# Linear attention and a sparse feed-forward layer: the gate products of token blocks two to four by two levels of seven products

## The chip, the cores and the metric

One core of one Trainium2 chip runs the kernel. The metric is the device time of one execution in microseconds (us); the kernel is run three times and the median is given. The engines are TensorE (PE in the profile; PEld are its weight loads), VectorE (DVE), ScalarE (ACT), GpSimd (POOL) and SyncE (SP), whose queue issues nearly all transfers. Each engine works through its instructions in the order in which they were written.

## The reference

Two stages with a residual each, on 2 x 1024 tokens of width 512, all in float32. The change is in the second.

```python
x = L0_attn_x                                     # (2, 1024, 512)
x = x + _layernorm(_L0_attn_ref(_layernorm(x), Wq, Wk, Wv, Wo))
x = x + _layernorm(_L0_ffn_ref(_layernorm(x), w_gate, w_up, w_down))

def _L0_ffn_ref(x, w_gate, w_up, w_down):         # (512, 2048), (512, 2048), (2048, 512)
    h = silu(einsum('bsh,hi->bsi', x, w_gate)) * einsum('bsh,hi->bsi', x, w_up)
    h_sparse = _sparsify_2to4(h)                  # of each 4 neighbours keep the 2 of largest |h|
    return einsum('bsi,ih->bsh', h_sparse, w_down)
```

`_L0_attn_ref` is a causal linear attention with 16 heads of 128 channels.

## The kernel before

The first 650 us are the attention, chunk by chunk of 128 tokens; the change leaves its code as it is. Then comes the feed-forward stage in four blocks of 512 tokens (`m` = 0 to 3; the text counts them from one). A block's hidden layer of 2048 is computed in four sets of 512 columns (`jb` = 0 to 3). For each set there is a `gate` and an `up`, both 512 x 512 x 512; after the four sets there is one `down`, 512 x 2048 x 512.

**Seven products.** Each of these matrix products is made by seven products of half the size in each direction in place of eight (a scheme of Strassen's kind). `FACTORS` says which of the seven combined weights meets which of the seven combined inputs. Three of the weight factors are quarters of the weight itself; the other four were summed ahead, by POOL in the attention stage, and lie in DRAM (`gu_dram`, `d_dram`). The inputs are combined by DVE and POOL (`ffn_input`, lines 1998 to 2005, tile `fxt`; `sparsify`, lines 1785 to 1794, tile `ht`).

`chain` (line 630) makes the seven products in the order 1, 2, 6, 5, 7, 4, 3. Products 1, 6, 7 and 4 add up in one PSUM bank (kind `b`); in between ACT copies the bank to SBUF (`snapshot`, line 659). Product 2 has a bank of kind `a`; 5 and 3 share one of kind `e`. DVE adds `a` or `e` to a snapshot to finish a quarter of the result (`added`, line 672). The fourth quarter is read from bank `b` itself. There are two banks of kind `a` and three each of `b` and `e`. For a gate or an up, one of the seven products is four matmuls with 128x128 weights and 256 moving columns (`project_ffn`, line 364); for a down it is sixteen (line 1811).

**After the products.** ACT applies Silu to the gate's quarters (`gate`, lines 1668 to 1678). `sparsify` multiplies gate and up on DVE, takes absolute values on ACT (line 1743), compares and counts on DVE (lines 1749 to 1775) and keeps two of four (line 1779), some 13 us of DVE for a set. The three differences of tile `ht` and one POOL sum (line 1794) make the factors for down.

**Order.** `Plan` orders the instructions. TensorE's are written out by hand in `ffn_order`; everything else is a process that names its engine and a length in us (`yield "dve", 0.7`), and the plan simulates them and writes each engine's instructions in the order it found. Lengths are constants: that one engine slows another is not in them. `weave` alternates between a gate and an up of the same or the next set. In down, products 1, 2 and 5 are split: part one uses sets 0 to 2, part two set 3, which is selected last.

**Between blocks.** Before, all seven products of the second block's first gate are run within or right after the first block's last gate and up products, or between the parts of down. At the change from the second block to the third no gate product stands between them, and at the next change two do. The input of block `m` is normalized one block ahead (`ffn_normalized`), transposed by DVE and through DRAM (`ffn_input`, `fb_dram`), and held in two tiles that alternate (`xs`, `xo`), so that it is loaded a block ahead.

**Buffers.** `ring` holds 12 gate or up factors of 256 KB each; `wd` holds 4 down factors of 1024 KB; `fx` holds the blocks' residual inputs until the output is written (`write_output`).

Of the kernel before, what the change touches and what calls it, by code (L numbers as in the profile page):

```python
# [17 lines left out]
P = 128  # L18
# [201 lines left out]
def layer(  # L220
# [47 lines left out]
    gu_dram = [[dram.tile([P, 4, 512], F32, name=f"{of}s{jb}") for of in "gu"] for jb in range(NJB)]  # L268
    d_dram = dram.tile([P, NJB, 4, 512], F32, name="d_dram")
# [53 lines left out]

    def load_x2(m):
# [18 lines left out]
    def load_gu(jb, which, i):  # L343

        t = pool["ring"].tile([P, 2, 2, P], F32, tag="gu", name="wgu")
        f = FACTORS[i][0]
        h, m = QUARTERS[f]
        if f < 3:
            of = columns((w_gate, w_up)[which], jb)
            v = of.rearrange("p (h k) (j m c) -> p h k j m c", h=2, j=2, m=2)  # L350
        else:
            of = gu_dram[jb][which]
            v = of.rearrange("p (h k) (j m c) -> p h k j m c", h=2, j=2, m=2)
        for k in range(2) if f < 3 else [slice(0, 2)]:
            nc.sync.dma_start(out=t[:, k], in_=v[:, h, k, :, m, :])
        return t
# [21 lines left out]
    def down_factor(i):  # L378
        wi = FACTORS[i][0]
        w = pool["wd"].tile([P, NJB, 2, 256], F32, tag="wd", name="wd")  # L380
        h, m = QUARTERS[wi]
        if wi < 3:
            of = w_down.rearrange("(b p h k) (m c) -> p b h k m c", b=NJB, h=2, k=2, m=2)
        else:
            of = d_dram.rearrange("p b (h k) (m c) -> p b h k m c", h=2, m=2)
        for k in range(2):
            nc.sync.dma_start(out=w[:, :, k], in_=of[:, :, h, k, m, :])
        return w
# [241 lines left out]
    def chain(name, shape, length, product, names, keeps, c11, c12, c22, c21, last=None):  # L630
# [113 lines left out]
        plan.signal((*name, 3))  # L744
        yield
# [708 lines left out]

    def begin_ffn():

        for name, bufs in (("ring", 12), ("fx", 4), ("ln", 4), ("xs", 1), ("keeps", 4), ("s", 2)):
# [7 lines left out]
        first_ups = [(0, i) for i in ORDER] + [(1, i) for i in ORDER[:5]]  # L1465

        def first_gates():
# [3 lines left out]
            for jb, i in first_ups:  # L1471
                wgu_loaded.add((0, jb, 1, i))
                yield from load_factor(0, jb, 1, i)

        def normalized():
            yield 6.0
            scales = yield from layernorm_pair(ffn["x"], 4, "f4", None)
            for tt in range(4):
                yield "dve", 0.56
                xn = pool["ln"].tile([P, NIC, P], F32, tag="ln", name="fxn")  # L1480
                normalize(xn.rearrange("p c d -> p (c d)"), ffn["x"][tt], *scales[tt])
                ffn["xn"][tt] = xn
# [5 lines left out]
    def ffn_transposed(tt, kind):  # L1488
# [4 lines left out]
        pt, name = transposed(ffn["xn"][tt], kind, ("fxn", tt))  # L1493
# [34 lines left out]
    def load_factor(m, jb, which, i):  # L1528
        before, name = ring("gu", 12)
        yield from before  # L1530
        if FACTORS[i][0] > 2:
            yield "unit", 5 + 2 * jb + which
        yield "sp", 0.88 if FACTORS[i][0] < 3 else 0.44, 2
# [770 lines left out]
```

## Time and profile before

| | |
|---|---|
| median of three runs | 1267.67 us (1266.99 to 1269.98) |
| the profiled execution's time | 1267.78 us |
| its span, first to last instruction | 1266.1 us |
| granted TensorE clock | 0.998 |
| first gate product, last matmul group begins | 664.95 us, 1252.68 us |
| transfers | 252.60 MB, mean 200 GB/s |

The groups of lines that the change is near, from the list of the costliest groups (columns: line, engine, operation, tile written <- tiles read, shape, count | busy us, mean ns of one | idle before, and what ended it):

```profile
L364 PE MATMUL cb<-fxt,wgu 128*128 128x256 f32 x512 | 116.7, 380 | 1.0 <-ACT u L659 0.6
L659 ACT COPY u<-cb 128x512 f32<-128x512 f32 (+1 forms) x252 | 126.5, 502 | 432.9 <-PE cb L364 157.6
L1794 POOL TENSOR_TENSOR h<-h 128x512 f32<-128x512 f32 x16 | 26.1, 1636 | 303.2 <-DVE ht L1791 123.6
wgu<-gs SPq DMA_DIRECT2D x64, 256.0 KB, 3.6
wgu<-us SPq DMA_DIRECT2D x64, 256.0 KB, 3.1
wd<-d_dram SPq DMA_DIRECT2D x32, 512.0 KB, 5.0
```

A float32 matmul leaves two records, so 512 records of line 364 are 256 matmuls. Records overlap: the mean of one (380 ns) is from its start to its last result, and the next has begun before. What one costs is read from start to start.

### The profile page before, as it was taken

The numbers are of one execution on the slowest core, as the hardware profiler recorded it, in microseconds if no ns is written. First come the engines' busy times: TensorE is split into PE (matmuls) and PEld (weight loads), VectorE is DVE, ScalarE is ACT, GpSimd is POOL, SyncE is SP. The second block draws the span as 40 slices with busy tenths as digits, with TensorE's granted clock in tenths as the row PEclk, the third lists the DMA queues.
The fourth block names the chain that finished last, engine by engine and source line by source line (L and its number), as shares of the span: only waits on it lengthen the run. The fifth ranks groups of instructions, "written<-read, shape, count | busy, mean of one in ns | idle before, by whom it ended". The sixth has DMA issues, their size and how long they took to land. (4 is left out here: it accounts for less than half of the span.)

```text
span 1266.1 us, 17832 instructions
## 1 busy us (share of the span) xinstructions
PE 1247.5 (99%) x6092; PEld 990.1 (78%) x6092; DVE 850.9 (67%) x1577; ACT 464.5 (37%) x911; POOL 336.5 (27%) x263
## 2 busy tenths in 40 slices
PE   7999999999999999999999999999999999999998
PEld 4666776777767776777688888888888888888886
DVE  6898877876666677777764499227872698237763
ACT  3664454443443444444543333013411333023211
POOL 4554443332422455455421110010100101010010
PEclk9999999999999999999999999999999999999999
DMA  7377867769758776766575688376547775565312
GB/s 267 109 229 255 270 187 238 236 221 291 230 187 262 250 238 229 243 203 223 185 230 167 179 228 233 116 218 207 156 149 211 230 198 146 166 181 169 108 42 92
DMA packets 280297, 252.60 MB, mean 200 GB/s; under 512 B 19216, under 2 KB 239376, under 8 KB 277520
## 3 DMA queue, kind: packets, MB, share of 16 engines
q1 hardware_dynamic: 278832, 249.51, 63.6%
q10 hardware_dynamic: 1376, 1.97, 0.4%
q8 instruction: 49, 0.80, 0.3%
q14 instruction: 40, 0.33, 0.1%
HBM read 179.83 MB, written 71.57 MB: 199 GB/s over the span
## 5 line engine op out<-in xcount | busy, mean ns | idle before, releaser
L659 ACT COPY u<-cb 128x512 f32<-128x512 f32 (+1 forms) x252 | 126.5, 502 | 432.9 <-PE cb L364 157.6
L1234 ACT ACTIVATE o<-nm,den 128x128 f32<-128x128 f32 x256 | 81.5, 367 | 120.4 <-DVE den L1228 81.1
L1331 PE MATMUL cb<-wo,of 128*128 128x256 f32 x512 | 123.5, 384 | 0.6 <-ACT u L659 0.6
L883 PE MATMUL cb<-wq,xf 128*128 128x512 f32 x256 | 121.9, 598 | 0.0
L928 POOL TENSOR_TENSOR qraw<-qraw,r 128x512 f32<-128x512 f32 x48 | 62.8, 1308 | 213.7 <-DVE qraw L919 163.6
L364 PE MATMUL cb<-fxt,wgu 128*128 128x256 f32 x512 | 116.7, 380 | 1.0 <-ACT u L659 0.6
L364 PE MATMUL cb<-fxnT,wgu 128*128 128x256 f32 x512 | 116.8, 379 | 0.0
L1331 PEld LDWEIGHTS cb<-wo,of 128*128 128x128 f32 x512 | 93.6, 190 | 21.1 <-issue 8.2
L364 PEld LDWEIGHTS cb<-fxt,wgu 128*128 128x128 f32 x512 | 97.0, 190 | 15.1 <-ACT u L659 1.3
L364 PEld LDWEIGHTS cb<-fxnT,wgu 128*128 128x128 f32 x512 | 97.2, 190 | 13.3
L1794 POOL TENSOR_TENSOR h<-h 128x512 f32<-128x512 f32 x16 | 26.1, 1636 | 303.2 <-DVE ht L1791 123.6
L565 POOL TENSOR_TENSOR wraw<-wraw 128x512 f32<-128x512 f32 x68 | 95.5, 1404 | 2.4
L672 DVE TENSOR_TENSOR y<-u,ce 128x256 f32<-128x256 f32 (+1 forms) x42 | 18.9, 451 | 97.8 <-ACT u L659 65.0
L883 PEld LDWEIGHTS cb<-wq,xf 128*128 128x128 f32 x256 | 47.2, 190 | 44.7 <-issue 42.8
L883 PEld LDWEIGHTS cb<-wkv,xf 128*128 128x128 f32 x256 | 48.0, 192 | 31.7 <-issue 25.3
L883 PE MATMUL cb<-wkv,xf 128*128 128x256 f32 x256 | 68.2, 389 | 0.0
L1331 PE MATMUL ce<-wo,of 128*128 128x256 f32 x256 | 60.5, 379 | 0.0
L883 PE MATMUL ce<-wq,xf 128*128 128x512 f32 x128 | 60.2, 592 | 0.0
L364 PE MATMUL ca<-fxnT,wgu 128*128 128x256 f32 x256 | 58.8, 379 | 0.0
L364 PE MATMUL ce<-fxt,wgu 128*128 128x256 f32 x256 | 58.7, 379 | 0.0
L364 PE MATMUL ce<-fxnT,wgu 128*128 128x256 f32 x256 | 58.7, 379 | 0.0
L1811 PE MATMUL cb<-wd,h 128*128 128x256 f32 x256 | 57.3, 379 | 0.0
(189 smaller groups left out, 2415.6 us busy)
## 6 DMA issues: line engine op xcount, KB each, us to landing
wgu<-gs SPq DMA_DIRECT2D x64, 256.0 KB, 3.6
wgu<-us SPq DMA_DIRECT2D x64, 256.0 KB, 3.1
wd<-d_dram SPq DMA_DIRECT2D x32, 512.0 KB, 5.0
qb<-blocks SPq DMA_DIRECT2D x59, 256.0 KB, 2.3
qT<-qb SPq DMA_DIRECT2D x236, 64.0 KB, 2.6
ob<-blocks SPq DMA_DIRECT2D x58, 256.0 KB, 3.2
of<-ob SPq DMA_DIRECT2D x232, 64.0 KB, 2.5
xf<-xf SPq DMA_DIRECT2D x16, 896.0 KB, 5.4
```

Source lines behind the costliest of these rows:

```text
L364: nc.tensor.matmul(bank[:, j, :].rearrange("p (w t) -> p w t", t=32), w[:, k, j, :], xf[xi][:, k], start=(start and j == 0 and k == 0), st ...
L565: nc.gpsimd.tensor_tensor(to, i0, i1, op)
L659: nc.scalar.copy(kept[i], b)
L672: nc.vector.tensor_tensor(dst[:, rows], kept[i][:, rows], b, ALU.add)
L883: nc.tensor.matmul(bank.rearrange("p h d -> p (h d)"), xf[n][:, xi, k, :], w[wi][:, k, :], start=(start and k == 0), stop=(k == 1), skip_g ...
L928: nc.gpsimd.tensor_tensor(u, u, r, ALU.add)
L1234: nc.scalar.activation(t[:, u, :], nmv[:, u // 2, u % 2, 0:HD], AF.Copy, scale=den[:, u // 2, u % 2 : u % 2 + 1],)
L1331: nc.tensor.matmul(bank.rearrange("p h d -> p (h d)"), of[n, xi][:, k, :], weights[gp][2][wi][:, k, :], start=(start and k == 0), stop=(k ...
L1794: nc.gpsimd.tensor_tensor(b12, b22, b12, ALU.subtract)
L1811: nc.tensor.matmul(b[:, j if row is None else 0, :], hts_or_h(m, jb, hi)[:, k, j * P : (j + 1) * P], w[:, jb, k, :], start=(start and part ...
```

## The change

For the gates of blocks two to four (12 of 16) each of the seven products is made by seven products again: `inner_gate` uses `chain_of_chains` in place of `chain`. A product that was four matmuls of 256 columns becomes seven matmuls of 128 columns, their results in two PSUM banks (four in the first, three in the second). Snapshots and sums of the outer level hold seven 128-column results in place of four (tile `u2`, three buffers). When an outer quarter is complete, POOL makes its four inner quarters from the seven results by five additions (`post`); Silu follows.

The inner combinations of the weights are made by POOL from the outer factors: in block one, as the third and fourth gate's factors are loaded there, and for the first and second set after them (`inner_weights`, `more_inner_weights`); they are stored to DRAM (`gi_dram`), and an inner gate loads three quarters of the outer factor and the four inner sums, 448 KB in place of 256. The inner combinations of the input are 12 more DVE instructions per block (`inner`).

For their room other buffers are cut: `ring` holds 7 up factors and 4 larger gate factors, `wd` holds 3, and the fifth down factor is loaded to the two `fx` tiles; these no longer keep the residual, which is loaded again just before it is added (`residual`). The transposed input has one buffer, so it is loaded after the last gate and up product of the block before. `ht` has two places: its third difference overwrites the second after down's product 6. In `sparsify` the sums of the comparisons are reordered and partly written over the comparisons. Between blocks, eight of down's steps now run first, then the next gate's products 1 and 2 with down's last two between, then the first of the next up.

```diff
+    gi_dram = [dram.tile([P, 7, 4, P], F32, name=f"gi{jb}") for jb in range(NJB)]
...
+        if some:
+            nc.sync.dma_start(out=to[:, 0, 0, :], in_=v[:, 0, 0, :])
+            nc.sync.dma_start(out=to[:, 1], in_=v[:, 1])
+            return
...
+        t = pool["ring"].tile([P, 8, P], F32, tag="gi", name="wgi", bufs=GI)
+        v = t[:, 0:4].rearrange("p (k j) c -> p k j c", k=2)
+        load_blocks(v, jb, which, i, inner)
+        if inner:
+            nc.sync.dma_start(out=t[:, 4:8], in_=gi_dram[jb][:, FACTORS[i][0]])
+            return t
+        return v if which else (t[:, 4:8], v)
...
+        if i == 5:
+            ts = []
+            for b in range(2):
+                t = pool["fx"].tile([P, B, DM], F32, tag="fx", name="fx")
+                t = t.rearrange("p b (k c) -> p b k c", k=2)
+                for k in range(2):
+                    nc.sync.dma_start(out=t[:, :, k], in_=of[:, 2 * b : 2 * b + 2, h, k, q, :])
+                ts += [t[:, 0], t[:, 1]]
+            return ts
...
+    SLOTS = (1, 2, 6, 5, 7, 4, 3)
+    PARTS = (slice(0, 4), slice(4, 7))
...
+        def multiply(bs, i, start, more=None):
+            for part, (b, _, before) in enumerate(bs):
+                plan.pe(
+                    (0.89, 0.67)[part],
+                    partial(product, b, i, part, start),
+                    *names(i),
+                    *(before if start else [(*name, *more, part)]),
+                )
+            plan.signal((*name, i))
...
+        def snapshot(bs, i, last=False):
+            yield from taken(i)
+            for part, of_ in enumerate(PARTS):
+                yield "act", (0.62, 0.5)[part], 0
+                src = bs[part][0] if part == 0 else bs[part][0][:, 0:3]
+                nc.scalar.copy(kept[i][:, of_], src)
+                plan.signal(bs[part][1] if last else (*name, "kept", i, part))
+            if last:
+                yield from post(i, quads[i])

+        def added(i, bs, last):
+            for part, of_ in enumerate(PARTS):
+                yield (*name, "kept", i, part)
+                yield "dve", (0.73, 0.6)[part], 0
+                t = kept[i][:, of_]
+                src = bs[part][0] if part == 0 else bs[part][0][:, 0:3]
+                nc.vector.tensor_tensor(t, t, src, ALU.add)
+                plan.signal(bs[part][1] if last else (*name, "e", part))
+            yield from post(i, quads[i])
+
+        def post(i, quad):
+            begin, d, then = quad
+            yield from begin
+            d = d()
+            if i == 1:
+                plan.signal((*name, "begun"))
+            t = kept[i]
+            for length, to, i0, i1 in (
+                (0.8, d[:, 0], t[:, 0:1].broadcast_to([P, 2, P]), t[:, 1:3]),
+                (0.5, d[:, 1, 1], d[:, 0, 1], t[:, 4]),
+                (0.5, d[:, 1, 0], d[:, 1, 1], t[:, 5]),
+                (0.8, d[:, :, 1], d[:, :, 1], t[:, 3:4].broadcast_to([P, 2, P])),
+                (0.5, d[:, 0, 1], d[:, 0, 1], t[:, 6]),
+            ):
+                yield "pool", length
+                nc.gpsimd.tensor_tensor(to, i0, i1, ALU.add)
+            plan.signal(free[i])
+            yield from then()
...
+        b = banks("b")
+        multiply(b, 1, True)
+        plan.spawn(snapshot(b, 1))
+        yield
+        a = banks("a")
+        multiply(a, 2, True)
+        plan.spawn(added(1, a, True))
+        yield
+        multiply(b, 6, False, ("kept", 1))
+        plan.spawn(snapshot(b, 6))
+        yield
+        e = banks("e")
+        multiply(e, 5, True)
+        yield
+        multiply(b, 7, False, ("kept", 6))
+        plan.spawn(snapshot(b, 7))
+        plan.spawn(added(7, e, False))
+        yield
+        multiply(b, 4, False, ("kept", 7))
+        plan.spawn(snapshot(b, 4, True))
+        yield
+        multiply(e, 3, False, ("e",))
+        plan.spawn(added(6, e, True))
...
+    def inner_weights(jb, i, v, done):
+
+        t, v = v
+        yield "gu", 0, jb, 0, i
+        (a11, a21), (a12, a22) = ([v[:, k, j, :] for j in range(2)] for k in range(2))
+        s4, s2, s3, s1 = (t[:, k] for k in range(4))
+        for to, i0, i1, op in (
+            (s1, a21, a22, ALU.add),
+            (s2, s1, a11, ALU.subtract),
+            (s3, a11, a21, ALU.subtract),
+            (s4, a12, s2, ALU.subtract),
+        ):
+            yield "pool", 0.5, 2
+            nc.gpsimd.tensor_tensor(to, i0, i1, op)
+        yield "sp", 0.44, 2
+        nc.sync.dma_start(out=gi_dram[jb][:, FACTORS[i][0]], in_=t)
+        yield plan.transfer(256)
+        done()
+        plan.signal(("gi", jb, i))
+
+    def more_inner_weights():
+        yield "g", 0, 3, 7
+        for jb in range(2):
+            for i in ORDER:
+                t, name = yield from take("keep2", 3, new_keep2)
+                if FACTORS[i][0] > 2:
+                    yield "unit", 5 + 2 * jb
+                yield "sp", 0.88 if FACTORS[i][0] < 3 else 0.44, 2
+                v = t[:, 0:4].rearrange("p (k j) c -> p k j c", k=2)
+                load_blocks(v, jb, 0, i)
+                plan.spawn(landed(plan.transfer(256), ("more", jb, i)))
+                plan.spawn(inner_weights(jb, i, (t[:, 3:7], v), partial(plan.signal, name)))
...
-            if m == 0:
-                run(g, 4)
-            else:
-                g = gate(m + 1, 0)
-            if m != 1:
-                for part in range(2):
-                    run(products, 1)
-                    run(g, 1)
-            run(products, 8 if m == 1 else 6)
-            u = up(m + 1, 0)
-            for part in range(2):
-                if m == 1:
-                    run(g, 1)
-                run(u, 1)
-                run(products, 1)
-            live += [u] if m == 0 else [g, u]
+            run(products, 8)
+            g, u = gate(m + 1, 0), up(m + 1, 0)
+            run(g, 1)
+            run(products, 1)
+            run(g, 1)
+            run(products, 1)
             begin(m + 1)
+            run(u, 1)
+            live += [g, u]
...
+    def load_fifth(m):
+        for tt in range(4):
+            yield "fxn", min(m + 1, NM - 1), tt
+        yield from load_down_factor(m, 5, ("wd more", m))
...
+        def product(bank_, i, part, start):
+            w, name = wgu[m, jb, 0, i]
+            xi = FACTORS[i][1]
+            x_ = xfs[m][xi]
+            o_ = (0, 1, 3, 4, 5, 2, 6)[xi]
+            places = SLOTS[PARTS[part]]
+            for n, j in enumerate(places):
+                wj, xj = FACTORS[j]
+                if xj < 3:
+                    k, t_ = ((0, 0), (1, 0), (1, 1))[xj]
+                    rhs = x_[:, k, 4 * t_ : 4 * t_ + 4]
+                else:
+                    rhs = xis[m][:, xj - 3, o_].rearrange("p (w t) -> p w t", t=32)
+                nc.tensor.matmul(
+                    bank_[:, n, :].rearrange("p (w t) -> p w t", t=32),
+                    w[:, (0, 2, 3, 5, 4, 6, 7)[wj], :],
+                    rhs,
+                    start=(start and n == 0),
+                    stop=(n + 1 == len(places)),
+                    skip_group_check=True,
+                )
+            if part:
+                del wgu[m, jb, 0, i]
+                plan.signal(name)
...
+                1: (before, quad(0, 0, new), first_rows),
+                6: (begun, quad(0, 1), rows),
+                7: (begun, quad(1, 1), c22),
+                4: (begun, quad(1, 0), c21),
...
-        n = pool["m"].tile([P, 4, 512], BF16, tag="n", name="n")
-        for k, first, second, op in (
-            (0, g0[:, 0, :], g0[:, 1, :], ALU.add),
-            (0, n[:, 0, :], g0[:, 2, :], ALU.add),
-            (1, g1[:, 0, :], g0[:, 0, :], ALU.subtract),
-            (1, n[:, 1, :], g1[:, 1, :], ALU.add),
-            (2, g2, g0[:, 1, :], ALU.subtract),
-            (2, n[:, 2, :], g1[:, 0, :], ALU.subtract),
-            (3, g2, g1[:, 1, :], ALU.add),
-            (3, n[:, 3, :], g0[:, 2, :], ALU.add),
+        n0 = pool["m"].tile([P, 512], BF16, tag="n", name="n")
+        n = [n0, g0[:, 0, :], g0[:, 1, :], g2]
+        for to, first, second, op in (
+            (n[0], g0[:, 0, :], g0[:, 1, :], ALU.add),
+            (n[0], n[0], g0[:, 2, :], ALU.add),
+            (n[1], g1[:, 0, :], g0[:, 0, :], ALU.subtract),
+            (n[2], g2, g0[:, 1, :], ALU.subtract),
+            (n[3], g2, g1[:, 1, :], ALU.add),
+            (n[1], n[1], g1[:, 1, :], ALU.add),
+            (n[2], n[2], g1[:, 0, :], ALU.subtract),
+            (n[3], n[3], g0[:, 2, :], ALU.add),
...
-        t = pool["h"].tile([P, 3, 2, 256], F32, tag="ht", name="ht")
-        hts[m, jb] = [b11, b21, b22, t[:, 0], t[:, 1], b12, t[:, 2]]
-        for k, i0, i1 in ((0, b12, b11), (1, b22, t[:, 0]), (2, b21, t[:, 1])):
+        t = pool["h"].tile([P, 2, 2, 256], F32, tag="ht", name="ht")
+        hts[m, jb] = [b11, b21, b22, t[:, 0], t[:, 1], b12, t[:, 1]]
+        for k, i0, i1 in ((0, b12, b11), (1, b22, t[:, 0])):
             yield "dve", 0.7
             nc.vector.tensor_tensor(t[:, k], i0, i1, ALU.subtract)
         plan.signal(("ht", m, jb))
+
+        def third():
+            yield "d", m, 6
+            yield "dve", 0.7
+            nc.vector.tensor_tensor(t[:, 1], b21, t[:, 1], ALU.subtract)
+            plan.signal(("ht4", m, jb))
+
+        plan.spawn(third())
...
-            if m > 1:
-                yield "gu done", m - 2
+            yield "gu done", m - 1
             for b in range(4):
                 yield "sp", 0.44
                 if not xnT:
-                    of_ = pool["xs" if m % 2 == 0 else "xo"]
-                    xnT.append(of_.tile([P, 16, NIC, 32], F32, tag="fxnT", name="fxnT"))
+                    xnT.append(pool["xs"].tile([P, 16, NIC, 32], F32, tag="fxnT", name="fxnT"))
...
+        def inner(o_, count, part):
+            to = [
+                xis[m][:, k, o_ : o_ + count].rearrange("p i (w t) -> p i w t", t=32)
+                for k in range(4)
+            ]
+            for k, i0, i1 in (
+                (0, part(0, 1), part(0, 0)),
+                (1, part(1, 1), to[0]),
+                (2, part(1, 1), part(0, 1)),
+                (3, part(1, 0), to[1]),
+            ):
+                yield "dve", 0.15 + count * 0.15, 0
+                nc.vector.tensor_tensor(to[k], i0, i1, ALU.subtract)
+            plan.signal(("fxi", m, o_ // 2))
...
-        fxs[0] = ffn["x"]
         actx.close()
-        for name, bufs in (("wd", 4), ("h", 4), ("m", 1), ("y", 1), ("blocks", 2), ("xo", 1)):
+        for name, bufs in (("wd", 3), ("h", 4), ("m", 1), ("y", 1), ("blocks", 2), ("xi", 1), ("keep2", 3)):
```

## The prediction

> **What bounds the kernel now.** I read the page first, its busy times, then the costliest groups of TensorE.
>
> ```profile
> PE 1247.5 (99%) x6092; PEld 990.1 (78%) x6092; DVE 850.9 (67%) x1577; ACT 464.5 (37%) x911; POOL 336.5 (27%) x263
> PE cb L364 <- ACT u L659: 0.6, 1, 0.6
> PE cb L364 <- issue: 0.4, 1, 0.4
> ```
>
> The first line is the page's; the other two are all that TensorE waited for from 640 us to the end. From the first gate product (665 us) on, TensorE waits for about 1 us in all. So a TensorE time removed comes off the end in full, unless something else becomes late. What could be late is told by the second view: DVE's busy time in the stretch of each token block that starts when its first set of 512 hidden columns reaches the 2-of-4 selection and ends when the last set is selected (the fourth L1779 instruction). Columns: stretch, length, PE, PEld, DVE, ACT, POOL busy.
>
> ```profile
> 724.00:794.70 70.70, 70.28 (x326) 61.39 (x325) 64.74 (x100) 21.55 (x31) 6.23 (x4) 1.00 0.81 223
> 866.00:935.70 69.70, 69.70 (x325) 61.36 (x324) 64.59 (x108) 24.65 (x33) 5.58 (x3) 1.00 0.52 154
> 1000.00:1081.20 81.20, 81.20 (x378) 71.49 (x377) 71.30 (x116) 25.14 (x35) 6.02 (x4) 1.00 0.63 174
> 1145.00:1225.40 80.40, 80.40 (x374) 70.77 (x373) 61.33 (x96) 21.78 (x31) 5.07 (x3) 1.00 0.33 95
> ```
>
> DVE fills 92, 93, 88 and 76% of them while POOL does almost nothing. The page's 67% hides this. Part two of the first down product needs that selection; it starts at 802.68, 936.52, 1085.01 and 1226.60 us (timeline), so DVE has 8.0, 0.8, 3.8 and 1.2 us in hand.
>
> **TensorE: what is removed.** The third view is TensorE's timeline at a gate product (16 records of 256 columns) and where 128x128 weights meet 129 columns.
>
> ```profile
> 879.54 3.62 PE L364 MATMUL cb<-fxt,wgu 128*128 128x256 f32 x16
> 883.00 3.62 PE L364 MATMUL ce<-fxt,wgu 128*128 128x256 f32 x16
> 400.99 0.61 PE L1196 MATMUL nm<-state,qT 128*128 128x129 f32 x4
> 401.43 0.61 PE L1196 MATMUL nm<-mid,qT 128*128 128x129 f32 x4
> ```
>
> A float32 matmul leaves two records. From start to start, 256 columns take 3.46/16 = 0.216 us a record. Four records of 129 columns take 0.61 us, the last of them 0.275 (its row), so (0.61-0.275)/3 = 0.112; for 128 columns 0.111. A gate had 7 x 4 matmuls, 56 records, 12.10 us. It gets 49 matmuls of 128 columns, 98 records, 10.88 us. Saved: 1.22 us x 12 gates = 14.6 us. Bounds: 13.4 at 0.112; 17.0 at 0.109, the spacing of the 128-column transposes.
>
> [...]
>
> **DVE and POOL: what is added.** Per inner gate DVE adds 384 columns thrice, in between 0.41 us (a 128x256 sum from PSUM) and 0.69 us (128x512): 0.55 each, 1.65. Three gates end in a stretch: 5.0. Out of it go a third factor of `ht` for three sets, now made later (0.6 us each, start to start: -1.9), and about 1.0 from the selection's reordered sums, whose dependent pairs start 0.45 us apart and the others 0.34. Net +2.1.
>
> POOL sums each of four quarters with two instructions of 256 and three of 128 columns. A 128x512 sum of POOL's own takes 1.27 us, so 128 columns cost 0.32 to 0.42 (with the 0.10 us of the smallest memset): 0.37, and 256 columns 0.68. That is 2.47 a quarter, 9.9 a gate, 29.7 us in three gates. POOL alone has room for it: 11.2 of 23 us with the sum it has already. But the rows say what DVE pays:
>
> ```profile
> 1081.42 1.68 POOL L1794 TENSOR_TENSOR h<-h 128x512 f32<-128x512 f32 x1 [10.32 <-DVE ht L1791]
> 1080.57 0.69 DVE L1791 TENSOR_TENSOR ht<-h 128x512 f32<-128x512 f32 x1
> 1081.29 2.37 DVE L1791 TENSOR_TENSOR ht<-h,ht 128x512 f32<-128x512 f32 x2
> 901.06 4.31 POOL L1794 TENSOR_TENSOR h<-h 128x512 f32<-128x512 f32 x2 [42.16 <-ACT u L659]
> 902.04 2.20 DVE L1749 TENSOR_TENSOR g<-s 128x1536 bf16<-128x1536 f32 x1 [0.55 <-ACT s L1743]
> 904.16 0.67 DVE L672 TENSOR_TENSOR s<-u,ca 128x512 f32<-128x512 f32 x1
> 904.76 1.69 DVE L1754 TENSOR_TENSOR g<-s 128x1024 bf16<-128x1024 f32 x1
> ```
>
> Beside one POOL sum two DVE instructions take 2.37 us in place of 1.26, POOL 1.68 in place of 1.27. Beside two, L1749 takes 2.20 for 1.75 and L1754 1.69 for 1.22, while the one that reads PSUM keeps its 0.67. So DVE loses 1.1 us per 1.27 us of POOL's own (0.87), or 0.92 per 2.54 (0.36) in a stretch with idle time and a PSUM read. DVE works on two SBUF operands for some 12.6 of a set's 23 us (55%); 0.87 x 55% = 0.48. I take 0.42, between 0.36 and 0.48: 12.5 us in a stretch. Bounds: nothing, if POOL runs only beside PSUM reads and idle time, and 0.87 throughout, 25.8 us.
>
> [...]
>
> So 14.6 us more DVE work stand in a stretch, while TensorE gets through three gates 3.7 us sooner: 18.3 us of room are used up. What room there is:
> - Block two (866 us): idle 5.1, in hand 0.8, two transposes of the next input that can go later 1.3: 7.2. Late by 11.
> - Block three (1000 us): idle 9.9, in hand 3.8, the next block's factors (L2002, 3.0) now made later, less two gate products (3.45) that stood between the parts of down: 13.3. Late by 5.
> - Block four: idle 19.1, in hand 1.2, less 2.1 in which only ACT's L1743 is awaited: 18.2. Late by 0.
> - Block one has outer gates still, but POOL makes inner weights: 14 factors x 4 x 0.37 = 20.7 us, x 0.42 = 8.7 on DVE, and some 1.5 for the further fourteen. Moved out: the next input's factors 3.1, two gate sums 1.3, `ht` and the selection 2.9. Net +2.9. Room: 6.0 + 8.0, less the seven gate products of block two (12.1) that stood before part two of down and now come later: 1.9. Late by 1.
>
> That is 17 us. TensorE's instructions wait in order, so lateness is not made up. ACT gets 3 x 0.46 and one 128x512 copy more per gate, and is under 40% busy: nothing.
>
> **Transfers and order.** A gate product's load grows from 256 to 448 KB; with the up product's 256 that is 704 KB in 3.28 us, 215 GB/s. A slice of the page reaches 291, so I take nothing; at the 173 GB/s mean of this half it would be 0.8 us a pair, 67 us. SP issues three transfers for an inner factor and one or two for an up factor, 4.4 x 0.45 = 2.0 of 3.28 us. The residual's reloads and the inner weights' stores go through SP too; its queue has that room. New waits: the fifth down factor uses the input's buffers, so its load is queued behind the next input's normalization on DVE and needs 5.0 us (wd's median) to land, before the third down product, 10.4 us after down begins; and the next input's transposed loads wait for the last gate and up product, then 3.6 us, then DVE's first four inner differences (1.8), before a gate at 34.6 us into down. Both hide unless DVE is late, and then they come next. The fourth quarter of `up` waits for two copies (1.05), POOL's sums (2.5), ACT's Silu (0.63) and a product on DVE (0.69), 4.9 us after its gate's product 4, and its bank is next used six products, 9.8 us, after that. No row prices these together: 0 to 15, and I take 6, two per inner block, nearer to the end where each is covered. PSUM banks now go in pairs; the nearest reuse leaves an up product and half a gate product, 2.5 us, and stays under the 6.
>
> **The sum.** -14.6 + 17 + 6 = +8.4 us. The profiled execution took 1267.78 us, its span 1266.1; the median of the runs is 1267.67, so nothing need be carried over: 1276. All at the low ends: -17, 1251; POOL's price at 0.87: 13.3 more in each of blocks two to four and 9.3 in block one, their room being used up: +8.4 + 49.2 = +58, 1325.
>
> **Rivals.**
> - *DVE keeps up* (faster). POOL's sums fall beside PSUM sums and idle time; then 2.1 + 3.7 is inside every room and 14.6 us come off: 1253, up to 1262 with a few waits. For it: block four has 19 us idle, and PSUM readers lose nothing. Against: 29.7 us don't fit beside 5 us idle in block two.
> - *A cancellation.* DVE's loss is 0.36 and the waits hide: block two late by 9, three by 3, then 12 - 14.6, about 1265. The measurement of this kernel tells 0.3%, 3.8 us, from no change.
> - *Weight loads bind* (slower). If 128-column records went at 0.15 us, as the 34.1 us over 224 records of L1196 taken as a mean would have it, a gate would take 14.9 us: +33, 1301. The 0.112 us rows speak against; that mean holds the tails of each group. It decides from 0.123 us a record, where 98 records cost what 56 did.
> - *The weights come late* (slower): 67 us at the worst, 1335; the 291 GB/s slice speaks against.
>
> **How the numbers follow.** Forecast (DVE beside POOL makes down wait): 0.55, own range 1272 to 1305. DVE keeps up 0.28; cancellation 0.11; weight loads 0.04; late weights 0.02. Faster 0.28, same 0.11, slower 0.61. The range 1253 to 1303 leaves out about one in twenty below, and of the slower cases the far end, one in ten.
>
> **What would show it.** Records of 128 columns 0.11 us apart in the gates; L1749, L1754 and the selection's other SBUF instructions 20 to 50% longer in blocks two to four, L672 unchanged; POOL near 10 us a gate before contention; TensorE idle before part two of the first down product, longest in block two. Wrong if DVE's instructions keep their length, if that gap is absent, or if TensorE waits on DMA or at the gates' own banks instead.

## The result and the profile after

| | before | after |
|---|---|---|
| median | 1268.6 us (4 runs, 1266.99 to 1269.98) | 1290.36 us (4 runs, 1288.61 to 1290.88) |
| ratio | | 1.0172, 95% interval 1.0157 to 1.0187 |
| span of the profiled execution | 1266.1 us | 1288.3 us |

The change costs 21.8 us where +8.4 was forecast. The direction was right, and the time lies inside the range (1253 to 1303), but by luck: most of the 21.8 us is a wait that the sum did not contain.

Two lines of the page of the kernel after: TensorE's busy time, and the granted clock in 40 slices of 32 us.

```profile
PE 1238.8 (96%) x6596; PEld 993.7 (77%) x6596; DVE 921.6 (72%) x1649; ACT 487.9 (38%) x967; POOL 567.1 (44%) x615
PEclk9999999999999999999999999699999999999999
```

TensorE has less to do than before (1247.5) in a longer span: the time went to waits. One slice, the 26th (805 to 837 us), has a lower clock. The longest of TensorE's waits from 640 us on in the kernel after (three more come to 2.5 us; columns: line waited for; us in total, times, longest):

```profile
PE cb L2060 <- DMA wd<-d_dram: 20.4, 2, 20.2
PE cb L1858 <- ACT u L804: 4.7, 3, 1.8
PE ce L382 <- DVE h L699: 2.2, 3, 0.7
PE ca L382 <- DVE u L815: 1.2, 1, 1.2
```

Before, all of them came to 1 us. Now they come to 31, and nearly two thirds of that is a single wait, for a transfer, in down (L2060) of block one. TensorE's timeline there:

```profile
800.27 1.89 PE L2060 MATMUL ce<-fx,ht 128*128 128x256 f32 x8
822.38 1.19 PE L2060 MATMUL cb<-wd,h 128*128 128x256 f32 x2 [20.23 <-DMA wd<-d_dram]
823.76 4.44 PE L2060 MATMUL cb<-wd,h 128*128 128x256 f32 x12 [0.18 <-DMA wd<-d_dram]
```

The awaited tile is down's factor 7. There are three `wd` buffers; factor 7 takes that of factor 1, whose last record begins before 791.6 us (there TensorE goes on to `ca`, product 2). When was its load issued? Parts of SyncE's timeline in the kernel after (L1684 stores an inner weight, L360 loads gate and up weights, L2249 loads the transposed input, L414 is the load of `wd`):

```profile
786.87 1.02 SPq L360 DMA_DIRECT2D u<-in_w_gate_dram  x2
790.93 0.34 SPq L1684 DMA_DIRECT2D gi<-u  x1
...
798.85 0.94 SPq L360 DMA_DIRECT2D u<-in_w_gate_dram  x2
802.60 0.34 SPq L1684 DMA_DIRECT2D gi<-u  x1
802.98 1.14 SPq L360 DMA_DIRECT2D u<-in_w_gate_dram  x2
804.17 1.94 SPq L2249 DMA_DIRECT2D fxnT<-fb  x4
808.39 0.34 SPq L1684 DMA_DIRECT2D gi<-u  x1
...
814.88 1.20 SPq L414 DMA_DIRECT2D wd<-d_dram  x2
```

The load went out 23 us after its buffer came free. Ahead of three of these stores the queue stands still: from 787.9 to 790.9, from 799.8 to 802.6, from 806.1 to 808.4. Earlier stores had held it too: from 769 us to the issue of the load SyncE stands still ahead of stores for 22 us in all. Much of the 23 us then goes to issuing what had piled up: 36 transfers, 15.7 us. The longest of SyncE's waits from 760 to 830 us:

```profile
SPq L1684 <- POOL u L1682: 17.7, 8, 3.3
SPq L1684 <- DMA u<-in_w_gate_dram: 6.1, 2, 5.1
SPq L1684 <- POOL wgi L1682: 5.0, 2, 4.5
```

So the stores wait for 28.8 us in these three lines alone, and 22.7 of them are put down to POOL's inner sums (L1682). And POOL waits for the loads that stand on SyncE behind the stores:

```profile
800.76 3.16 POOL L1682 TENSOR_TENSOR u<-u 128x128 f32<-128x128 f32 x7 [4.77 <-DMA u<-gs]
806.97 2.22 POOL L1682 TENSOR_TENSOR u<-u 128x128 f32<-128x128 f32 x5 [3.04 <-DMA u<-in_w_gate_dram]
813.90 2.17 POOL L1682 TENSOR_TENSOR u<-u 128x128 f32<-128x128 f32 x3 [4.71 <-DMA u<-gs]
```

It is a loop of load, sum and store over three buffers, on two engines that each worked in order (from 799.8 to 802.6 us SyncE issued nothing, with the store at 802.60 next), and the load of factor 7 stands in the middle of it. The wait has a tail. Busy time in the wait and after it (columns: stretch, length, PE, PEld, DVE, ACT, POOL busy, granted clock, DMA share, GB/s):

```profile
803.00:822.40 19.40, 0.01 (x1) 0.04 (x1) 7.38 (x12) 0.00 (x0) 11.09 (x20) 0.59 0.76 227
822.40:826.90 4.50, 4.32 (x9) 2.98 (x10) 3.02 (x7) 0.00 (x0) 1.41 (x2) 0.50 1.10 342
826.90:860.00 33.10, 31.30 (x171) 27.58 (x170) 7.50 (x17) 5.49 (x10) 7.50 (x14) 1.00 0.87 277
```

For 4.5 us after it the clock is 0.50, and the records lie 427 ns apart in place of 216: 2.6 us more, a short wait for the factor's second half included. During the wait 227 GB/s moved, and 342 in the next stretch: it is not bandwidth that lacked. Nor were the loads slow once issued: the six loads `u<-gs` of 256 KB issued between 780 and 826 us landed after 4.0 us (median), where `wgu<-gs` took 3.6 before.

The whole account comes from TensorE's records: how far each start lies behind the one before, beyond the usual 215.9 ns for 256 columns and 111.5 ns for 128. From the first gate to the end that surplus was 1.9 us before and is 38.0 after. Of the 38.0, 23.0 are this wait and its tail; 2.2 stand at 842 to 845 us, about half of it for the next factor's load; 10.5 lie in the gates and ups of blocks two to four, 4.5, 3.5 and 2.5 a block; the rest are small. Surplus +36.1 and span +22.2 leave 13.9 us that TensorE saved.

### The profile page after: what moved, and what is told of

Same layout as the page of the kernel before. It is cut to its first block, busy times and chain, and to the rows that moved or that the text cites. A ratio compares the mean times of both kernels' runs of the same rounds, so it can differ in the third digit from the quotient of the medians.

```text
span 1288.3 us, 19538 instructions
## 1 busy us (share of the span) xinstructions
PE 1238.8 (96%) x6596; PEld 993.7 (77%) x6596; DVE 921.6 (72%) x1649; ACT 487.9 (38%) x967; POOL 567.1 (44%) x615
## 4 chain that ended last, share of the span: by engine, by line
PE 69%; DVE 17%; DMA 5%; ACT 3%; POOL 3%; issue 2%; SPq 2%; ACTq 0%; DVEq 0%; POOLq 0%
PE cb L999 12%; PE cb L1447 8%; PE cb L2060 7%; PE ce L999 5%; PE cb L382 4%; PE ce L1447 4%; PE nm L1312 3%; PE ce L2060 3%; PE ca L999 3%; DVE g L2016 3%; PE nm L1323 3%; PE ce L382 2%; PE sc L1198 2%; PE cb L1858 2%; PE ca L1447 2%
## 5 line engine op out<-in xcount | busy, mean ns | idle before, releaser
L686 ACT COPY u<-cb 128x512 f32<-128x512 f32 (+1 forms) x216 | 105.6, 489 | 368.7 <-PE cb L2060 126.9
L834 POOL TENSOR_TENSOR s<-s,u 128x128 f32<-128x128 f32 x192 | 126.7, 662 | 14.2
L834 POOL TENSOR_TENSOR s<-u 128x256 f32<-128x256 f32 x48 | 38.0, 793 | 116.6 <-DVE u L815 116.6
L2060 PE MATMUL cb<-wd,h 128*128 128x256 f32 x256 | 60.4, 392 | 20.4 <-DMA wd<-d_dram 20.4
L2060 PEld LDWEIGHTS cb<-wd,h 128*128 128x128 f32 x256 | 49.2, 195 | 29.8 <-POOL u L1682 20.6
L699 DVE TENSOR_TENSOR y<-u,ce 128x256 f32<-128x256 f32 (+1 forms) x42 | 18.8, 450 | 68.8 <-ACT u L686 42.9
L804 ACT COPY u<-cb 128x512 f32<-128x512 f32 x96 | 49.8, 531 | 36.4 <-PE cb L1858 31.2
L382 PE MATMUL cb<-fxnT,wgu 128*128 128x256 f32 x256 | 60.5, 379 | 0.0
L382 PE MATMUL cb<-fxt,wgu 128*128 128x256 f32 x240 | 57.0, 380 | 0.8 <-ACT u L686 0.7
L1052 DVE SCALAR_TENSOR_TENSOR qraw<-qraw,r 128x512 f32<-128x512 f32 x48 | 41.2, 858 | 22.0 <-ACT r L1049 21.8
L2060 PE MATMUL cb<-wd,ht 128*128 128x256 f32 x256 | 56.9, 380 | 0.0
```

The costliest lines, as they stand in the source:

```text
L382: nc.tensor.matmul(bank[:, j, :].rearrange("p (w t) -> p w t", t=32), w[:, k, j, :], xf[xi][:, k], start=(start and j == 0 and k == 0), st ...
L686: nc.scalar.copy(kept[i], b)
L804: nc.scalar.copy(kept[i][:, of_], src)
L834: nc.gpsimd.tensor_tensor(to, i0, i1, ALU.add)
L1052: nc.vector.scalar_tensor_tensor(f, u, 0.0, r, ALU.max, ALU.add)
L2060: nc.tensor.matmul(b[:, j if row is None else 0, :], hts_or_h(m, jb, hi)[:, k, j * P : (j + 1) * P], w[jb][:, k, :], start=(start and part ...
```

## The experiments

Each was timed beside the kernel before on the same chip, and the ratio is to that. In the first four runs its median was 1267.49 us.

**Set two's inner sums later.** In `more_inner_weights`:

```diff
         for jb in range(2):
             for i in ORDER:
+                if jb:
+                    yield "wd", 0, 7
```

> The seven inner weight sums of set two start only when down's factor 7 of block one has landed; nothing else is edited. If SP's queue is the cause (the load of factor 7, whose buffer came free at 791.6 us, was issued at 814.9 behind stores that wait for POOL), the 20.2 us wait before down's product 7 and the 2.6 us of lower clock after it go: about 1267 us. If the transfers themselves are too slow there, the same bytes have to move and 10 us or more of the wait stay: 1277 or above. If DVE beside POOL is the cause, as was predicted, nothing much changes: 1285 to 1290.

Measured: 1289.56 us, ratio 1.0169 (1.0153 to 1.0184). The wait for factor 7 is still 15.5 us: its load is issued at 812.06, behind stores of set one at 789.81, 799.35 and 807.61, which I had thought would be done by then. Some 4 us of new waits appear, as set two's weights come late. Moving half of the work behind the load does not free the queue, and puts a cost elsewhere.

**The stores on POOL's own queue.**

```diff
-        nc.sync.dma_start(out=gi_dram[jb][:, FACTORS[i][0]], in_=t)
+        nc.gpsimd.dma_start(out=gi_dram[jb][:, FACTORS[i][0]], in_=t)
```

> All 28 stores of inner weight sums are issued from POOL's own queue in place of SP's, so that SP waits for none of them. SP's queue as the cause: the wait before down's product 7 of block one goes as in the kernel above, 1264 to 1268 us, less what POOL pays for issuing (28 issues, unknown, off the path while POOL has room). Transfers too slow: the wait stays, 1285 or above.

Measured: 1283.46 us, 1.0122 (1.0106 to 1.0138). The wait shrinks to 10.6 us, and the load is issued at 809.42. SyncE now waits at its loads for the stores to land, since the buffers come free only then:

```profile
SPq L360 <- DMA gi<-u: 21.2, 8, 5.4
```

The loop is shorter and still holds the queue.

**Sets one and two left out.** Their sums, loads and stores are not made; their gates read the inner weights of sets three and four.

> Leaves out the inner weight sums of sets one and two (loads, 56 POOL sums, 14 stores); the gates of these sets read the sums of sets three and four. Both SP's queue and slow transfers as the cause let the wait before down's product 7 go: 1264 to 1267 us. It is the floor for any other order of this step: if the two kernels above come within 2 us of it, order alone was the cost, and the step itself is hidden. If it stays above 1280, the cause is not in this step.

Measured: 1267.29 us, 0.9988 (0.9977 to 0.9999). The wait is gone with its tail, and the time is that of the kernel before: the 14 units at this place cost 23 us.

**Two sums for five.** The first edit, and POOL makes each quarter with two sums of 256 columns; three of the inner sums are left out of the result.

```diff
-                (0.5, d[:, 1, 1], d[:, 0, 1], t[:, 4]),
-                (0.5, d[:, 1, 0], d[:, 1, 1], t[:, 5]),
-                (0.8, d[:, :, 1], d[:, :, 1], t[:, 3:4].broadcast_to([P, 2, P])),
-                (0.5, d[:, 0, 1], d[:, 0, 1], t[:, 6]),
+                (0.8, d[:, 1], t[:, 3:4].broadcast_to([P, 2, P]), t[:, 4:6]),
```

> The first of these kernels (set two's sums after factor 7), and POOL makes an outer quarter with two sums of 256 columns in place of five instructions; the other three inner sums are left out, 4.9 in place of 10.7 us of POOL's own a gate. If DVE beside POOL makes the 11 us of waits inside the gate and up products of blocks two to four (at 900, 923, 942, 1067, 1086, 1211, 1229 us), DVE's two-operand instructions there shorten, the waits go in the main and the time falls by 6 to 11 us below the first kernel: about 1257. If these waits come from the order of the queues alone, they stay: within 3 us of the first kernel.

Measured: 1279.56 us, 1.0095 (1.0078 to 1.0112), 10.0 us below the first edit alone, with 16.4 us of the wait for factor 7 still there. So the waits in the gates are a second cost, and POOL's sums make it.

**Three loads on ScalarE's queue.** This was to be the clean test of order against transfers.

```diff
+        queue = nc.scalar if m == 0 and i in (7, 4, 3) else nc.sync
...
-            nc.sync.dma_start(out=w[:, :, k], in_=of[:, :, h, k, q, :])
+            queue.dma_start(out=w[:, :, k], in_=of[:, :, h, k, q, :])
```

> Down's factors 7, 4 and 3 of token block one are issued from ScalarE's queue in place of SyncE's; the inner sums, their loads and their stores stay where they are. If SyncE's order is the cause (the load stands behind stores that wait for GpSimd), the load starts within 3 us of the buffer coming free (about 793 us), the 20.4 us of idle TensorE and the 2.6 us of lower clock behind it go, and the time is 1264 to 1269. If the transfers are too slow (the new traffic fills the DMA engines), the load is issued early but lands late, 10 us or more of the wait stay, and the time is 1277 or above. If the loads of block one only make room for a wait on the next ones (factors of block two, gate weights of sets one and two), some 4 to 8 us of new waits stand between 820 and 900 us and the time is 1270 to 1276.

Measured: 1296.18 us, 1.0213 (1.0196 to 1.0231), slower still. ScalarE's timeline:

```profile
800.89 1.27 ACTq L415 DMA_DIRECT2D wd<-d_dram  x2
802.20 0.59 ACT L687 COPY u<-cb 128x512 f32<-128x512 f32 x1 [21.11 <-DMA u<-in_w_gate_dram]
```

The load did not start within 3 us of its buffer, but at 800.89, 8 us after. The program gives its transfers, whatever their queue, eight semaphores in turn in their written order (100 to 107 in this trace), and one that takes a semaphore waits until its last transfer is done: in the trace of the kernel after, none of the 1397 transfers that take one again is issued before that. For this load, with number 107, that was a piece of the transposed input that SyncE issued at 797.47 (the releaser in the line is inferred, and names a neighbour). So it was still behind SyncE; and ScalarE stood idle with it, the snapshot of bank `cb` behind it, which TensorE needed. What TensorE waited for:

```profile
PE cb L2061 <- POOL h L2044: 10.7, 1, 10.7
PE cb L2061 <- ACT u L687: 8.4, 1, 8.4
```

The second wait is that snapshot. The first is POOL's sum for down's factors (tile `h`), which stood on POOL behind inner sums that waited for their loads. The time falls into "1277 or above", but not for that reading's reason: none of the three expectations described it.

**The same, with ScalarE's snapshots forward, and with two sums for five.** In the first the plan counts each quarter 0.8 us longer (`yield 0.8` before `plan.signal(free[i])`); in the second three of the inner sums are left out, as above.

> As the run before, and the plan counts each quarter of GpSimd's sums 0.8 us longer, so that the next gate's snapshot is put ahead of the Silu on ScalarE where it was behind it. If the waits of some 11 us inside the inner gates come from that order (a Silu that waits for a quarter drawn out by VectorE holds the next snapshot), the 1.9 us waits go and the time is 3 to 6 us below the run before. If they come from the sums' duration itself (banks and buffers come free late whatever the order), it is within 1.5 us of it. If the plan's longer quarters push down's second parts back, it is 1 to 3 us above.

> As the run with the three loads on ScalarE's queue, and GpSimd makes each quarter with two sums of 256 columns in place of five; three of the inner sums are left out of the result. If contention of GpSimd with VectorE and ScalarE makes the waits that are left, it is 8 to 11 us below that run (1254 to 1259), what TensorE's saving of about 14 us gives with hardly a wait. If the waits left are TensorE's own (banks, weights), less than 3 us of them go.

Measured: 1295.0 us, 1.0208 (1.0191 to 1.0225), within 1.5 us of the run before; and 1289.97 us, 1.0166 (1.0148 to 1.0184), 6.2 us below it, where 8 to 11 were expected. Both still carry waits at block one's down, 18.1 and 16.5 us in all, so they say little of the gates.

**The sums in place.** Sets one and two's inner weights are made like those of the other two sets, from the tiles that block one's own gates have just used. No second load, no sums beside down.

```diff
-        if m == 0 and which == 0 and jb > 1:
+        if m == 0 and which == 0:
...
-            used[jb, i]() if (which, m) == (0, 0) and jb > 1 else plan.signal(name)
+            used[jb, i]() if (which, m) == (0, 0) else plan.signal(name)
...
-        plan.spawn(more_inner_weights())
```

> The inner weights of sets one and two are summed in block one, in the tiles that its own gates have just used, as sets three and four are; their second load of 14 weights and the sums beside down go. All is computed. If the cost lies in where the 14 units stand (in the in-order queues of SyncE, GpSimd and ScalarE, ahead of down's factor 7), the stall of 20.4 us and the 2.6 us of lower clock behind it go, the waits of some 11 us inside the gates stay, and the time is 1264 to 1269, as in the run without these sums. If it lies in the amount of the work wherever it stands, the sums and stores, now at 620 to 700 us, make TensorE wait there, for the gate's weights above all, by 10 us or more, and the time is 1276 or above.

Measured: 1267.08 us, 0.9995 (0.9986 to 1.0004; before 1267.76), with everything computed. The same sums and stores, moved by some 140 us to where TensorE needed nothing from behind them, cost 22 us less. The load of factor 7 now goes out 21.7 us earlier, about as much as SyncE had stood still:

```profile
793.20 1.20 SPq L414 DMA_DIRECT2D wd<-d_dram  x2
```

What TensorE still waits for, and ScalarE's and POOL's timelines at the longest kind of it:

```profile
PE cb L1858 <- ACT u L804: 4.7, 3, 1.8
PE ce L382 <- DVE h L699: 3.8, 4, 1.8
PE cb L382 <- ACT u L686: 1.7, 3, 1.0
```

```profile
899.12 1.06 ACT L1826 ACTIVATE s<-s 128x1024 f32<-128x1024 f32 x1 [4.61 <-POOL s L834]
900.09 0.95 ACT L804 COPY u<-cb 128x512 f32<-128x512 f32 x2
```

```profile
895.77 3.31 POOL L834 TENSOR_TENSOR s<-s,u 128x128 f32<-128x128 f32 x4
899.05 1.72 POOL L2043 TENSOR_TENSOR h<-h 128x512 f32<-128x512 f32 x1
```

POOL ends a quarter at 899.05; ScalarE's Silu (L1826) waited 4.61 us for it, and the next gate's snapshots (L804) stand behind the Silu. TensorE, with an up product done at 898.8, waits 1.75 us for their bank.

**Three cures for the gates**, each on the sums in place: the longer quarters in the plan; the three 128-column sums of a quarter on VectorE; and the Silu alone held back in the plan (`if jb < 3: yield 2.0`).

> As the run with the sums in place, and the plan counts each quarter of GpSimd's sums 0.8 us longer, so that the next gate's snapshot is put ahead of the Silu on ScalarE where it was behind it. If the waits of some 1.9 us at the gates' banks come from that order, they go, and the time is 3 to 6 us below the run with the sums in place. If they come from the sums' own length (tiles and banks free late in any order), it is within 1.5 us of it.

> As the run with the sums in place, and the three sums of 128 columns of each quarter go to VectorE, the two of 256 stay on GpSimd. If the gates' waits come from GpSimd's length beside VectorE, a quarter is shorter (3 times 0.6 us of GpSimd against 3 times some 0.25 us of VectorE), the waits in the gates shrink, and the time is 2 to 6 us below the run with the sums in place. If VectorE's load is what counts there (it has 48 more sums a block, some 12 us), down's second part and the up sums come later and the time is 2 to 10 us above it.

> As the run with the sums in place, and the plan holds the Silu of the inner gates of sets one to three back by 2 us, so that the first snapshots of the fourth set's gate stand ahead of the third set's long Silu on ScalarE; nothing else is delayed by hand. If ScalarE's order makes the waits of 1.9, 1.9 and 1.4 us before the fourth set's gate, they go and the time is 4 to 6 us below the run with the sums in place (1261 to 1263), below the kernel before. If the wait only moves (to VectorE's sums of the up product, or to down's second part behind a later Silu), it is within 2 us of it.

Measured, beside 1267.08 for the sums in place (before 1267.76, for the third 1267.87):
- Longer quarters: 1268.98 us, 1.0018 (1.0007 to 1.0029), 1.9 above; neither reading foresaw that. In its profile the snapshot's waits are gone, and those for `h L699` rose from 3.8 to 6.1; but its runs spread from 1267.18 to 1273.39, and the profiled one is the slowest.
- VectorE for the short sums: 1266.82 us, 0.9994 (0.9984 to 1.0004): no difference that can be told. The snapshot's waits go here too, and ScalarE's own copies are late instead (`ACT u L686`, from 1.7 to 5.6).
- Silu held back: 1265.46 us, 0.9984 (0.9975 to 0.9992), some 1.7 below, which the two intervals do not tell from no difference. The wait moved, as the second reading had it:

```profile
PE cb L382 <- DVE h L1953: 4.2, 5, 1.1
PE ce L382 <- DVE h L699: 2.7, 3, 1.7
```

Where the snapshots stand first, the up product's bank waits for the product of Silu and up on VectorE (L1953). ScalarE's order decided where the wait stood, not whether there was one. This version has the lowest median of those that compute everything, some 2 us under the kernel before.

**What the gates' sums cost.** The sums in place, and two sums for five; three of the inner sums are left out of the result.

> As the run with the sums in place, and GpSimd makes each quarter with two sums of 256 columns in place of five; three of the inner sums are left out of the result. It bounds what is left of the change when hardly any GpSimd work stands in the gates: if their waits are the whole of what the run with the sums in place lacks of TensorE's saving, it is 8 to 11 us below that run (1256 to 1259). If VectorE's own load (selection, inner snapshots' sums) makes them, less than 4 us go.

Measured: 1256.22 us, 0.9901 (0.9888 to 0.9914), 11.0 us below the sums in place after each is set against its own run of before. TensorE's list is empty but for this and 0.2 us:

```profile
PE cb L382 <- ACT u L686: 1.8, 3, 0.7
```

So the waits in the gates come from POOL's sums, by their length and what they do to VectorE; the two were not separated.

## Why the prediction went wrong, point by point

The sum had three terms, -14.6 + 17 + 6. The runs give -11.7 (little left to wait for), +11.0 (the gates' waits) and +22.4 (the units beside block one's down), together the 21.8. The sign came out right by a term that the sum did not have: without it the change stands at -0.7, no difference that can be told.

- **The step that failed: "The residual's reloads and the inner weights' stores go through SP too; its queue has that room."** The queue's issues were counted in time, 2.0 of 3.28 us, and not in order. A store that waits for POOL holds everything behind it, and POOL waited for loads that stood behind stores. Shown: 20.2 us of wait with the load 23 us behind its buffer; without the 14 units, or with the same units 140 us earlier, it is gone and the time falls by 23 and 22 us. The prediction counted these units in block one, but only for what POOL's instructions take from VectorE. It also said that TensorE waiting on DMA would prove it wrong; that happened. The rival "the weights come late" (0.02) also had TensorE wait for transfers, but for others and for another reason: it priced bandwidth, at 215 GB/s against 291.
- **TensorE's saving: right.** Records of 128 columns lie 111.5 ns apart on average in the kernel after, those of 256 columns 215.9 before, so a gate takes 98 x 0.1115 = 10.93 us in place of 56 x 0.2159 = 12.09: 1.16 us, 14.0 for 12 gates, against 14.6. Every record has a full load of its own (6596 of each on the page), and none shows in the spacing: a load of the gates lasts 192 ns (median, L1858), and their records lie 111.5 apart. Of the 14.0 the last run kept 12.0 of span; its surplus of 2.9 us, 1.0 more than before, leaves 1 us that I can't place.
- **Down waiting for VectorE: the loss was there, not its effect (17 forecast, under 1 found).** VectorE's rows did lengthen as forecast, and the PSUM reader did not. In the kernel after, from 866 us on (columns: count, then busy us and mean ns):

```profile
L2016 DVE TENSOR_TENSOR g<-g,g 128x512 bf16<-128x512 bf16 x72 | 43.6, 654 | 0.4
L2020 DVE SCALAR_TENSOR_TENSOR h<-g,h 128x512 f32<-128x512 bf16 x36 | 29.0, 833 | 0.0
L699 DVE TENSOR_TENSOR h<-u,ce 128x512 f32<-128x512 f32 x24 | 16.2, 675 | 9.5 <-ACT u L686 4.9 <-PE ce L382 4.6
```

  Before, the same three took 419 to 425, 685 and 686 ns: 55% and 22% longer, and unchanged. POOL makes the difference, and not the new operands: six sums of the kernel after beside POOL, and six while POOL is idle:

```profile
912.62 4.20 DVE L2016 TENSOR_TENSOR g<-g,g 128x512 bf16<-128x512 bf16 x6
957.54 2.21 DVE L2016 TENSOR_TENSOR g<-g,g 128x512 bf16<-128x512 bf16 x6
```

  Counted against the same instructions with POOL idle, VectorE loses some 13.5 us in a stretch, where 12.5 was forecast. That this came so near is luck: POOL's new work is 41 us in three gates in place of 29.7, and VectorE loses 0.33 us for each of them in place of 0.42. Yet around part two of down TensorE's surplus is only 0.2 us in each of blocks two to four. What failed is the room. From the first set's selection to part two in blocks two to four of the kernel after (columns: stretch, length, PE, PEld, DVE, ACT, POOL busy, clock, DMA share, GB/s):

```profile
882.50:960.40 77.90, 74.23 (x456) 67.58 (x455) 71.32 (x99) 26.93 (x43) 45.95 (x60) 1.00 0.76 226
1025.90:1104.50 78.60, 76.12 (x470) 69.53 (x468) 71.71 (x99) 27.34 (x43) 46.19 (x60) 1.00 0.75 221
1169.70:1247.70 78.00, 76.05 (x470) 69.43 (x468) 71.26 (x99) 27.44 (x44) 45.51 (x60) 1.00 0.53 157
```

  Before, with the same bounds, they were 69.9, 85.4 and 82.0 us long, with VectorE busy for 65.0, 74.7 and 62.9. The forecast had each 3.7 us shorter; that of block two is 8 us longer. TensorE's waits in the gates are 4.5 us of it, but in the last run, whose gates hardly wait, it is still 74.8 us (857.66 to 932.47), so the new order makes a part. In block three VectorE does less in the stretch than before, although it loses 13.5 us there, so other work has left it. There was room for it in the whole round from part two to part two, where VectorE is now busy for 110.1 of 144.1 us in block three (94.8 of 148.5 before) and 102.4 of 143.2 in block four (76.1 of 141.6). The step that failed is taking the stretch as closed, in its length and in what stands in it.
- **The waits in the gates: right in kind, too small (6 forecast, 11 found), and in their place.** Of the chain that was named, quarter, Silu, product, bank, the first two steps make the longest waits, but through the order on ScalarE that ties one gate's Silu to the next gate's snapshot, which the sum did not have. The whole chain, down to the product on VectorE (L1953), ends waits only in the runs that put the snapshots ahead of the Silu (1.5, 2.0 and 4.2 us). It was priced with no contention, at 4.9 us against 9.8 of cover.
- **POOL's price: too low.** In the kernel after:

```profile
L834 POOL TENSOR_TENSOR s<-s,u 128x128 f32<-128x128 f32 x144 | 86.7, 605 | 10.4
L834 POOL TENSOR_TENSOR s<-s,u 128x256 f32<-128x256 f32 x48 | 40.0, 834 | 3.8
```

  The shortest of them, in the run with the sums in place, take 0.446 us (128 columns) and 0.722 (256), where 0.37 and 0.68 were taken: 2.8 us a quarter for 2.47, and (86.7 + 40.0 + 38.0, the other 256-column group) / 12 = 13.7 a gate with contention. The part of a sum that does not shrink with its columns is some 0.18 us, an estimate from these lengths and the 1.27 us of 512 columns before; the prediction gave it between nothing and 0.10.
- **What proved harmless:** the fifth down factor's load, the input's transposed loads, and the larger gate loads; none is among TensorE's waits. What the pairs of banks cost is not known: TensorE does wait for banks in the gates and ups.

That the order of the queues, not the transfers, makes the 20 us rests on SyncE's standstill, on the placing of the sums, and on the GB/s and the landing times in the wait. The two runs without the wait also move less, 14 loads of 256 KB, and the attempt to take the load alone out of the queue was not clean.

## What to carry to other kernels

A queue's room was here a matter of order (a load 23 us behind its buffer), not only of issue time (2.0 of 3.28 us): for each transfer that TensorE will need, list what stands ahead of it on its queue and what those wait for, and look for loops (a load behind a store that waits for an engine that waits for a load). Before background work is put beside a critical stretch, try to place it where its operands are already on the chip; that was worth 22 us here and cost no instruction. An engine's busy stretch that looked full said little of what added work would delay (VectorE lost some 13.5 us in one, and TensorE's surplus around part two of down was 0.2 us a block): follow which of the engine's instructions somebody waits for.

## What the hardware showed that was not expected

- After 20.2 us of idle TensorE the granted clock was 0.50 for 4.5 us, with 256-column records 427 ns apart in place of 216, and then 1.00 at once; it fell within the wait, whose mean is 0.59. The tail cost 2.6 us.
- A POOL sum of two float32 operands takes 0.45 and 0.72 us for 128 and 256 columns (the shortest with the sums in place) and 1.27 for 512 (before) undisturbed: a line with about 0.18 us at its foot, by an estimate from the three.
- Bfloat16 sums of two operands on VectorE (L2016) start 0.70 us apart beside POOL (six in 4.20 us); with POOL idle, their starts lay 0.40 apart on average before and 0.38 after.
